# A state-space mixer on one core: the work between two sequences spread over sixteen states, and the router's statistics taken in the mixer's last sequence

## The chip, the core and the metric

The kernel runs on one core of a Trainium2 chip. Five engines work side by side, each through its own queue of instructions in order: PE (TensorE, matrix products into PSUM), DVE (VectorE), ACT (ScalarE), POOL (GpSimd) and SP (SyncE, which here only issues DMAs). The metric is the device time of one execution in microseconds.

## The reference

Eight sequences of 512 tokens, 256 wide, go through four layers; each layer is an attention-like mixer and a feed-forward part, and each part is `x = x + layernorm(part(layernorm(x)))`. The change touches the mixer of the last layer (called L3_attn), and the first step of the part after it (L3_ffn, a mixture of eight experts). The mixer, with DI = 512 channels and 16 states:

```python
xr = x @ W_in.T
xc, res = (xr[..., :DI], xr[..., DI:])
u = silu(conv1d(xc, W_conv, taps=4, causal) + b_conv)        # per channel
x_dbl = u @ W_xproj.T                                        # -> dt (16), B (16), C (16)
delta = softplus(dt @ W_dt.T + b_dt)
A = -exp(A_log)                                              # 512 x 16
dA = exp(delta * A);  dBu = delta * B * u                    # per channel and state
h_t = dA_t * h_{t-1} + dBu_t                                 # scan over the 512 tokens
y = sum over states of h * C,  + u * D
return (y * silu(res)) @ W_out.T
```

The router of L3_ffn then works on `layernorm(x)`: `softmax(xf @ w_router)`, the best two of eight experts for each token.

## The kernel before, in words

A framework orders the instructions. The program is traced in Python, and when it ends, a scheduler plays it against a model of the chip and lays down one fixed queue for each engine. An instruction that stands earlier in the Python code goes first when two are ready at the same modelled moment; one that stands much later may be pulled far forward when its engine is idle in the model. On the chip nothing is reordered: an instruction at the head of a queue waits, and everything behind it on that engine waits too. `tc.keep_in_program_order(ins)` pins an instruction behind the one traced before it on its engine, and `tc.issue_after(ins)` pins a block's instructions behind `ins`. Tiles come from pools: a tile of a tag with `bufs` buffers can be written only when the tile that used the buffer `bufs` allocations ago is no longer read.

`l3_attn` (from line 1506) goes through 8 sequences (`b`) times 16 states (`n`) in one loop. For each state:

- `inputs(b, n)` (L1603) is called two states ahead. It loads C over a DMA, and makes dB = du * B for all four channel blocks. For even n, PE spreads B over the partitions into PSUM (tile `pb`, L1610) and DVE multiplies (L1613); for odd n, B comes over a DMA and POOL multiplies (L1618).
- Four times, ACT computes dA (L1664) into one of two PSUM buffers and DVE scans (L1667) into `h`; six `h` tiles of two blocks each exist, so three states.
- POOL multiplies the two `h` tiles by C (L1670).
- PE adds the products of the state before onto four PSUM accumulators (`summed`, L1638).

All other matrix results go through the two PSUM buffers of the pool `pmm`: `pb`, the input projections `pi` (L1546), the convolution `pc` (L1560), `px` (L1570), `pd` (L1583), the transposes `pxT` (L146) and the output projection `py` (L185).

What stands between two sequences (the boundary) is traced in state n = 0 of the new one. `gate` (L1628, DVE) multiplies the four accumulators with silu(res), in the tile `sr`. `out` (L1622) calls `project_out`, whose two PSUM tiles `py` are read first by `bn_stats` (DVE), and then, after the statistics, by the four normalizing activations `yn` (L172, ACT); POOL adds the result to X (L174). Then four projections give the new `sr`, copied to SBUF by ACT (L1682), and Silu is applied (L1683). The Silu needs another table in ACT than Exp and Ln do, so a table load comes before it and `log_exp_tables` (L124) puts the first table back.

`front(b + 1)` (L1551) is a generator that is advanced once a state, from n = 0: norm and transposes, four convolutions with one yield each, the Silu of u with its two table loads (L1565), `px`, four pieces of delta (`pd`, five ACT and three DVE instructions each, L1583 to L1596), and last du = delta * u, as one POOL instruction (L1599). The tile `yn` and the normalized tile `xn` (L160) share one buffer (tag `xn`).

In `l3_ffn`, `route(b)` begins with `K.norm(b)`, whose `stats` (L99) are four `bn_stats`, four `bn_aggr` and, outside the mixer, an inverse square root of thirteen small DVE instructions (L118, L90 to L96). In the mixer (`log_exp` set) Ln and Exp on ACT and three small DVE instructions (L111 to L115) do the same.

Of the kernel before, what the change touches and what calls it, by code (L numbers as in the profile page):

```python
# [9 lines left out]
F32 = mybir.dt.float32  # L10
# [3 lines left out]
AF = mybir.ActivationFunctionType  # L14
# [5 lines left out]
P = 128  # L20
# [25 lines left out]
class Kern:  # L46


    def __init__(self, ctx, tc, i):
        self.ctx, self.tc, self.nc, self.i = ctx, tc, tc.nc, i  # L50
        nc = self.nc
        self.const = ctx.enter_context(tc.tile_pool(name="const", bufs=1))
        self.xpool = ctx.enter_context(tc.tile_pool(name="xres", bufs=1))
        self.wpool = ctx.enter_context(tc.tile_pool(name="wts", bufs=1))
        self.small = ctx.enter_context(tc.tile_pool(name="small", bufs=3))
        self.dram = ctx.enter_context(tc.tile_pool(name="dram", bufs=1, space=DRAM))
        self.C = self.const.tile([P, 384], F32, name="C")
        nc.sync.dma_start(out=self.C, in_=i["consts"][:, 0:384])
        self.ident = self.C[:, C_ID:C_ID + 128]
        self.caus = self.C[:, C_CAUS:C_CAUS + 128]  # L60
        self.up = self.C[:, C_UP:C_UP + 128]
        self.ones = self.const.tile([1, 128], F32, name="ones")
        nc.vector.memset(self.ones, 1.0)
        self.XA = self.xpool.tile([P, NB, NT, D], F32, name="X")
        self.X = [self.XA[:, b] for b in range(NB)]
        self.W = {}

        self.log_exp = False
        self.eps = self.const.tile([P, 1], F32, name="eps")
        nc.vector.memset(self.eps, LN_EPS)  # L70
# [54 lines left out]

    def norm(self, b, pool):

        nc = self.nc
        x = self.X[b]
        mv, r = self.stats([x[:, n, :] for n in range(NT)], "ln")  # L130
        xn = pool.tile([P, NT, D], F32, tag="xn", name=f"xn{b}")
# [31 lines left out]

    def add_norm(self, b, ys, pool, tag="yn"):

# [3 lines left out]
        nc.vector.scalar_tensor_tensor(nb, mv[:, :, 0], -1.0, r, ALU.mult, ALU.mult)  # L169
        t = pool.tile([P, NT, D], F32, tag=tag, name=f"yn{b}")  # L170
        for n in range(NT):
            nc.scalar.activation(  # L172
                t[:, n, :], ys[n], AF.Identity, bias=nb[:, n:n + 1], scale=r[:, n:n + 1])
        nc.gpsimd.tensor_tensor(self.X[b], self.X[b], t, ALU.add)  # L174

    def project_out(self, b, chunks, psum, ptag, pool, tag="yn"):

        nc = self.nc
        ys = []
        for half in range(2):  # L180
            ps = psum.tile([P, 2, D], F32, tag=ptag, name=f"py{b}_{half}")
            for j in range(2):
# [5 lines left out]
                ys.append(ps[:, j, :])  # L188
        self.add_norm(b, ys, pool, tag)

# [1315 lines left out]
def l3_attn(K):  # L1506

    nc, tc = K.nc, K.tc  # L1510
    w = K.W["l3_attn"]
# [4 lines left out]
    with ExitStack() as es:  # L1516
# [33 lines left out]

        def front(b, res):  # L1551
            xT = K.norm_T(
# [3 lines left out]
            for c in range(4):  # L1556
# [7 lines left out]
                yield  # L1564
            nc.scalar.activation(flat(u), flat(u), AF.Silu)  # L1565
            K.log_exp_tables()
            yield
            px = pmm.tile([48, L], F32, tag="mm", name=f"px{b}")
# [10 lines left out]

            dl = s2.tile([P, 4, L], F32, tag="dl", name=f"dl{b}")  # L1580
            for c in range(4):
                ps = pmm.tile([P, L], F32, tag="mm", name=f"pd{b}_{c}")
# [13 lines left out]
                nc.vector.tensor_tensor(dl[:, c, :], ps, dl[:, c, :], ALU.add)  # L1596
                yield
            du = s2.tile([P, 4, L], F32, tag="du", name=f"du{b}")
            nc.gpsimd.tensor_tensor(flat(du), flat(dl), flat(u), ALU.mult)  # L1599
            res.update(xT=xT, u=u, dl=dl, du=du, xd=xd,  # L1600
# [21 lines left out]
        def out(b, yT):  # L1622
            K.project_out(
                b, [(yT[:, c, :], W[:, c, M_OUT:M_OUT + D]) for c in range(4)], pmm, "mm", s1, tag="xn")

# [5 lines left out]
        def summed(state):  # L1631
# [4 lines left out]
            for j, h in enumerate(hs):  # L1636
                for c in range(2):
                    nc.tensor.matmul(  # L1638
                        py[2 * j + c], lhsT=K.ident, rhs=h[:, c, :], start=False,
                        stop=(n == NS - 1))  # L1640

# [5 lines left out]
        py = sr = last = None  # L1649
        nxt = iter(())  # L1650
        for k, (b, n) in enumerate(order):
            if n == 0:
                nxt = front(b + 1, res[b + 1]) if b + 1 < NB else iter(())
                dl, u = res[b]["dl"], res[b]["u"]
# [17 lines left out]
            if n == 0:  # L1672
                yT = gate(b - 1, py, sr) if b else None
                py = [pY.tile([P, L], F32, tag=f"y{c}", name=f"y{b}_{c}") for c in range(4)]
                for c in range(4):
                    nc.tensor.matmul(
                        py[c], lhsT=dg[:, c, 4, :], rhs=u[:, c, :], start=True, stop=False)
                if b:
                    out(b - 1, yT)
                sr = s1.tile([P, 4, L], F32, tag="sr", name=f"sr{b}")  # L1680
                for c in range(4):
                    nc.scalar.copy(sr[:, c, :], project_in(b, 4 + c, res[b]["xT"]))  # L1682
                nc.scalar.activation(flat(sr), flat(sr), AF.Silu)  # L1683
                K.log_exp_tables()
            last = (py, hs, n)
            next(nxt, None)
        summed(last)
        out(NB - 1, gate(NB - 1, py, sr))
        K.log_exp = False

def l3_ffn(K):
# [18 lines left out]
    with ExitStack() as es:  # L1712
# [60 lines left out]
        def route(b, sb):  # L1773

            xn = K.norm(b, sb)
            nc.sync.dma_start(
# [342 lines left out]
```

## Time and profile before

| what | value |
|---|---|
| runs shown | 5260.04, 5270.05 and 5273.43 us, median 5270.05 |
| profiled execution, its own time | 5271.25 us |
| its span in the profile | 5269.5 us |
| mean granted TensorE clock | 0.926 |
| busy over the span | PE 84%, DVE 57%, ACT 36%, POOL 35% |
| the mixer's first du and its last addition to X (POOL) | start 3503.6 us and 4627.0 us |

Times in the profile are microseconds from the start of the span. A line of a timeline gives the start, the duration, the engine, the line of the kernel, the operation, the tile written and those read, how many such instructions were merged, and in brackets how long the engine had been idle before it and whose end released it. The shares of busy time are averages over stages with different limits, so the mixer is read by itself below, one sequence at a time.

### The profile page before, as it was taken

The page shows a single profiled execution, that of the slowest core. Times are in us where ns is not written, and L with a number is a line of the kernel's source. Part 1 is how long each engine was busy: PE and PEld are TensorE (multiplying, and loading weights), DVE is VectorE, ACT ScalarE, POOL GpSimd, SP SyncE. Part 2 cuts the span into 40 slices and gives each one's busy share as a digit, 9 for nine tenths or more (in the row PEclk, how much of TensorE's full clock was granted, in tenths as well). Part 3 has the DMA queues.
Part 4 walks back from the last instruction along what each step waited for, and adds up shares of the span by engine and source line. Part 5 has one row for each costly group of instructions (what it writes and reads, how often), then busy time and mean ns, then how long its engine had stood idle before and what let it go on. Part 6 is the DMA issues. An engine that isn't in the chain of part 4 may idle for free.

```text
span 5269.5 us, 56453 instructions
## 1 busy us (share of the span) xinstructions
PE 4444.4 (84%) x18804; PEld 2705.9 (51%) x18804; DVE 3024.7 (57%) x8229; ACT 1886.4 (36%) x3769; POOL 1866.9 (35%) x1201
## 2 busy tenths in 40 slices
PE   8755789999983996888888889978888888899998
PEld 3334675565652994444444445533333333368885
DVE  7999646476686114454554544347777777761114
ACT  5401324443441332333333332345555555421112
POOL 0001213443442443111111110037888778903331
PEclk9777889999996997999999999989999999899999
DMA  4297411000001992000000000011111111126763
GB/s 115 78 215 161 132 49 42 5 9 5 5 17 48 251 251 59 4 5 5 5 5 4 1 1 20 1 31 45 49 46 46 43 44 46 42 86 197 233 215 102
DMA packets 401527, 357.88 MB, mean 68 GB/s; under 512 B 209394, under 2 KB 334020, under 8 KB 400676
## 3 DMA queue, kind: packets, MB, share of 16 engines
q1 hardware_dynamic: 373236, 305.83, 21.0%
q0 software_dynamic: 16320, 31.65, 2.2%
q10 hardware_dynamic: 11680, 16.80, 1.0%
q8 instruction: 149, 2.44, 0.2%
q14 instruction: 142, 1.16, 0.1%
HBM read 287.87 MB, written 66.09 MB: 67 GB/s over the span
## 4 chain that ended last, share of the span: by engine, by line
PE 38%; DVE 16%; ACT 5%; POOL 4%; issue 4%; DMA 1%; POOLq 0%; DVEq 0%; ACTq 0%; SPq 0%
DVE h L1667 7%; PE gb L1746 4%; PE T L1402 4%; PE h L1234 3%; PE S L1379 3%; PE y L1638 3%; PE g L1495 3%; PE yb L1760 2%; DVE junk L1384 2%; DVE dB L1613 2%; PE py L185 2%; PE pc L1560 2%; PE y L1245 2%; PE o L1411 2%; ACT PT L1405 1%
## 5 line engine op out<-in xcount | busy, mean ns | idle before, releaser
L1670 POOL TENSOR_TENSOR h<-h,C 128x1024 f32<-128x1024 f32 x256 | 596.0, 2358 | 177.6 <-DVE h L1667 140.5
L1638 PE MATMUL y<-h,C 128*128 128x512 f32 x1024 | 533.4, 661 | 106.7 <-POOL h L1670 106.7
L1667 DVE TENSOR_TENSOR_SCAN h<-dA,dB 128x512 f32<-128x512 f32 x512 | 588.9, 1202 | 28.4 <-ACT dA L1664 11.7
L1664 ACT ACTIVATE dA<-dl,A 128x512 f32<-128x512 f32 x512 | 352.5, 691 | 411.1 <-DVE h L1667 395.3
L1638 PEld LDWEIGHTS y<-h,C 128*128 128x128 f32 x1024 | 202.8, 209 | 413.9 <-issue 226.6
L929 POOL TENSOR_SCALAR p<-p,rs 128x128 f32<-128x128 f32 (+3 forms) x256 | 276.3, 1089 | 386.9 <-DVE rs L928 227.2
L1379 PE MATMUL S<-KT,qz 128*128 128x512 f32 (+3 forms) x1024 | 348.9, 477 | 41.7 <-ACT qz L1367 21.3
L174 POOL TENSOR_TENSOR X<-X,yn 128x1024 f32<-128x1024 f32 x64 | 151.2, 2363 | 654.8 <-ACT yn L172 593.7
L1405 ACT ACTIVATE PT<-T 128x256 f32<-128x256 f32 (+3 forms) x512 | 211.8, 437 | 387.4 <-PE T L1402 379.7
L1402 PE MATMUL T<-qz,KT 128*128 128x512 f32 (+3 forms) x1024 | 313.9, 450 | 2.9 <-DVE mx L1384 0.3
L1407 POOL TENSOR_SCALAR_AFFINE_SELECT PT<-PT 128x512 f32<-128x512 f32 x128 | 81.6, 637 | 634.0 <-ACT PT L1405 630.5
L1379 PEld LDWEIGHTS S<-KT,qz 128*128 128x128 f32 x1024 | 183.5, 197 | 209.8 <-DVE mx L1384 57.8
L1618 POOL TENSOR_TENSOR dB<-du,B 128x2048 f32<-128x2048 f32 x64 | 289.8, 4529 | 0.1
L1384 DVE CUSTOM_DVE_ANT_0 junk<-S,mask 128x256 f32<-128x256 f32 (+3 forms) x512 | 250.2, 489 | 60.8 <-PE S L1379 15.3
L1746 PE MATMUL gb<-xbT,w_b 128*128 128x256 f32 (+1 forms) x1472 | 255.3, 332 | 1.0 <-ACT ts L1950 0.6
L1613 DVE TENSOR_TENSOR dB<-du,pb 128x2048 f32<-128x2048 f32 x64 | 145.4, 2273 | 170.4 <-PE pb L1610 120.7
L1746 PEld LDWEIGHTS gb<-xbT,w_b 128*128 128x128 f32 x1472 | 230.2, 191 | 23.1 <-ACT ts L1950 0.8
L1402 PEld LDWEIGHTS T<-qz,KT 128*128 128x128 f32 x1024 | 170.7, 192 | 133.9 <-issue 85.6
L1752 DVE TENSOR_TENSOR hTb<-sb,gb 128x512 f32<-128x512 f32 x71 | 48.8, 688 | 325.4 <-PE gb L1746 325.4
L927 ACT ACTIVATE p<-p,nm 128x128 f32<-128x128 f32 (+3 forms) x256 | 143.8, 563 | 196.8 <-DVE nm L923 191.9
L1239 ACT ACTIVATE hT<-h,w_l_ffn 128x128 f32<-128x128 f32 x384 | 109.8, 368 | 220.6 <-PE h L1234 220.6
L1234 PE MATMUL h<-xgT,w 128*128 128x128 f32 x1536 | 185.3, 279 | 0.0
(503 smaller groups left out, 9045.0 us busy)
## 6 DMA issues: line engine op xcount, KB each, us to landing
w_b<-l3f_w SPq DMA_DIRECT2D x138, 512.0 KB
w<-l1f_w SPq DMA_DIRECT2D x48, 1024.0 KB
C<-xdd SPq DMA_DIRECT2D x128, 256.0 KB
B<-xdd SPq DMA_DIRECT2D x64, 256.0 KB
w<-l1f_w SPq DMA_DIRECT2D x48, 256.0 KB
toep<-l0fd SPq DMA_DIRECT2D x32, 320.0 KB
X<-x SPq DMA_DIRECT2D x16, 512.0 KB
toep<-l0fd SPq DMA_DIRECT2D x32, 256.0 KB
```

Source lines behind the costliest of these rows:

```text
L929: nc.gpsimd.tensor_scalar(p[:, 0:n], p[:, 0:n], rs, None, ALU.mult)
L1234: nc.tensor.matmul(ph[:, j, :], lhsT=w1[:, s, c, m * P:(m + 1) * P], rhs=xgT[:, c, :], start=(c == 0), stop=(c == 1))
L1379: nc.tensor.matmul(ps[:, 0:n], lhsT=QZ[:, j, qt * P:n], rhs=KT[:, g, 0:n], start=True, stop=True)
L1384: nc.vector.tensor_tensor_reduce(out=junk[:, 0:n], in0=tiles[j][:, 0:n], in1=mask[:, L - n:L], scale=1.0, scalar=-3.0e38, op0=ALU.add, op1 ...
L1402: nc.tensor.matmul(ps[:, 0:n], lhsT=KT[:, g, kt * P:(kt + 1) * P], rhs=QZ[:, j, kt * P:L], start=True, stop=True)
L1405: nc.scalar.activation(PT[:, j, :], ps[:, 0:n], AF.Exp)
L1618: nc.gpsimd.tensor_tensor(dB, du, B[:, None, :].to_broadcast([P, 4, L]), ALU.mult)
L1638: nc.tensor.matmul(py[2 * j + c], lhsT=K.ident, rhs=h[:, c, :], start=False, stop=(n == NS - 1))
L1664: nc.scalar.activation(dA, dl[:, c, :], AF.Exp, scale=A[:, c, n:n + 1])
L1667: nc.vector.tensor_tensor_scan(hs[-1][:, c % 2, :], dA, dB[:, c, :], 0.0, ALU.mult, ALU.add)
L1670: nc.gpsimd.tensor_tensor(h, h, C[:, None, :].to_broadcast([P, 2, L]), ALU.mult)
L1746: nc.tensor.matmul(ps[:, q, :], lhsT=ww[:, k, (c + q) * P:(c + q + 1) * P], rhs=xT[:, k, :], start=(k == 0), stop=(k == 1))
```

## The change

Six things are done, all in `l3_attn` but for the last.

1. The boundary's work becomes a generator, `among`, advanced once a state from n = 1 on: `out` in state 1, two of the four projections for `sr` in state 2 and two in state 3, then the pieces of `front(b + 1)` from state 4 on. `gate` and the first products onto the accumulators stay in state 0.
2. The Silu of `sr` stands directly before the Silu of u in `front`, with one return to the first table behind both. The yield behind them is gone.
3. Delta comes in two pieces to a state rather than one.
4. du is four POOL instructions of 128x512, each directly behind its piece of delta, rather than one of 128x2048.
5. The output projection's two PSUM tiles are copied to SBUF by ACT, and the normalizing activations read the copy.
6. In the last sequence, where there is no next `front`, the norm statistics that the router needs for sequences 0 to 6 are computed one to a state from state 5 on, each group behind a `memset` (the fence) that is pinned in program order, and kept in tiles of their own. `route` uses them.

```diff
+    def fence(self):
+        t = self.small.tile([P, 1], F32, tag="fence", name="fence")
+        return self.tc.keep_in_program_order(self.nc.vector.memset(t, 0.0)).ins
...
-        mv, r = self.stats([x[:, n, :] for n in range(NT)], "ln")
+        mv, r = known or self.stats([x[:, n, :] for n in range(NT)], "ln")
...
         t = pool.tile([P, NT, D], F32, tag=tag, name=f"yn{b}")
+        for n, ps in enumerate(halves):
+            nc.scalar.copy(t[:, 2 * n:2 * n + 2, :], ps)
+        if halves:
+            ys = [t[:, n, :] for n in range(NT)]
...
-            nc.scalar.activation(flat(u), flat(u), AF.Silu)
+            for t in (sr, u):
+                if t is not None:
+                    nc.scalar.activation(flat(t), flat(t), AF.Silu)
             K.log_exp_tables()
-            yield
...
-                yield
-            du = s2.tile([P, 4, L], F32, tag="du", name=f"du{b}")
-            nc.gpsimd.tensor_tensor(flat(du), flat(dl), flat(u), ALU.mult)
+                nc.gpsimd.tensor_tensor(du[:, c, :], dl[:, c, :], u[:, c, :], ALU.mult)
+                if c % 2:
+                    yield
...
+        def among(b, yT, sr):
+            if b:
+                out(b - 1, yT)
+            yield
+            sr.append(s1.tile([P, 4, L], F32, tag="sr", name=f"sr{b}"))
+            for c in range(4):
+                nc.scalar.copy(sr[0][:, c, :], project_in(b, 4 + c, res[b]["xT"]))
+                if c % 2:
+                    yield
+            if b + 1 < NB:
+                yield from front(b + 1, res[b + 1], sr[0])
+            else:
+                nc.scalar.activation(flat(sr[0]), flat(sr[0]), AF.Silu)
+                K.log_exp_tables()
+                for d in range(NB - 1):
+                    yield
+                    mv = K.const.tile([P, NT, 2], F32, name=f"fmv{d}")
+                    r = K.const.tile([P, NT], F32, name=f"fr{d}")
+                    K.known.append((mv, r))
+                    with tc.issue_after(K.fence()):
+                        m, t = K.stats([K.X[d][:, n, :] for n in range(NT)], "ln")
+                        nc.vector.tensor_copy(mv, m)
+                        nc.vector.tensor_copy(r, t)
...
-                if b:
-                    out(b - 1, yT)
-                sr = s1.tile([P, 4, L], F32, tag="sr", name=f"sr{b}")
-                for c in range(4):
-                    nc.scalar.copy(sr[:, c, :], project_in(b, 4 + c, res[b]["xT"]))
-                nc.scalar.activation(flat(sr), flat(sr), AF.Silu)
-                K.log_exp_tables()
+                sr = []
+                nxt = among(b, yT, sr)
+            else:
+                next(nxt, None)
             last = (py, hs, n)
-            next(nxt, None)
```

More of the change, by code (lines that the diff above doesn't have):

```diff
@@ L68, in __init__ @@
         self.log_exp = False
+        self.known = []
         self.eps = self.const.tile([P, 1], F32, name="eps")
@@ L124, in log_exp_tables, with norm @@
             self.nc.scalar.preload_act_table_set("natural_log_exp_and_others"))
[L126 removed]
+    def fence(self):
+        t = self.small.tile([P, 1], F32, tag="fence", name="fence")
+        return self.tc.keep_in_program_order(self.nc.vector.memset(t, 0.0)).ins
+    def norm(self, b, pool, known=None):
         nc = self.nc
         x = self.X[b]
[L130 removed]
+        mv, r = known or self.stats([x[:, n, :] for n in range(NT)], "ln")
         xn = pool.tile([P, NT, D], F32, tag="xn", name=f"xn{b}")
@@ L162, in norm_act, with add_norm @@
         return xn
-    def add_norm(self, b, ys, pool, tag="yn"):
+    def add_norm(self, b, ys, pool, tag="yn", halves=()):
         nc = self.nc
@@ L174, in add_norm, with project_out @@
         nc.gpsimd.tensor_tensor(self.X[b], self.X[b], t, ALU.add)
-    def project_out(self, b, chunks, psum, ptag, pool, tag="yn"):
+    def project_out(self, b, chunks, psum, ptag, pool, tag="yn", leave=False):
         nc = self.nc
-        ys = []
+        ys, halves = [], []
         for half in range(2):
@@ L188, in project_out @@
                 ys.append(ps[:, j, :])
-        self.add_norm(b, ys, pool, tag)
+            halves.append(ps)
+        self.add_norm(b, ys, pool, tag, halves if leave else ())
 def load_l0_attn(K):
@@ L1549, in project_in, with front @@
             return ps
-        def front(b, res):
+        def front(b, res, sr=None):
             xT = K.norm_T(
@@ L1580, in front @@
             dl = s2.tile([P, 4, L], F32, tag="dl", name=f"dl{b}")
+            du = s2.tile([P, 4, L], F32, tag="du", name=f"du{b}")
             for c in range(4):
@@ L1623, in out @@
             K.project_out(
-                b, [(yT[:, c, :], W[:, c, M_OUT:M_OUT + D]) for c in range(4)], pmm, "mm", s1, tag="xn")
+                b, [(yT[:, c, :], W[:, c, M_OUT:M_OUT + D]) for c in range(4)], pmm, "mm", s1, tag="xn",
+                leave=True)
         def gate(b, py, sr):
@@ L1649, in l3_attn @@
         py = sr = last = None
-        nxt = iter(())
         for k, (b, n) in enumerate(order):
             if n == 0:
-                nxt = front(b + 1, res[b + 1]) if b + 1 < NB else iter(())
                 dl, u = res[b]["dl"], res[b]["u"]
@@ L1672, in l3_attn @@
             if n == 0:
-                yT = gate(b - 1, py, sr) if b else None
+                yT = gate(b - 1, py, sr[0]) if b else None
                 py = [pY.tile([P, L], F32, tag=f"y{c}", name=f"y{b}_{c}") for c in range(4)]
@@ L1677, in l3_attn @@
                         py[c], lhsT=dg[:, c, 4, :], rhs=u[:, c, :], start=True, stop=False)
-                if b:
-                    out(b - 1, yT)
-                sr = s1.tile([P, 4, L], F32, tag="sr", name=f"sr{b}")
-                for c in range(4):
-                    nc.scalar.copy(sr[:, c, :], project_in(b, 4 + c, res[b]["xT"]))
-                nc.scalar.activation(flat(sr), flat(sr), AF.Silu)
-                K.log_exp_tables()
+                sr = []
+                nxt = among(b, yT, sr)
+            else:
+                next(nxt, None)
             last = (py, hs, n)
-            next(nxt, None)
         summed(last)
-        out(NB - 1, gate(NB - 1, py, sr))
+        out(NB - 1, gate(NB - 1, py, sr[0]))
         K.log_exp = False
@@ L1773, in route @@
         def route(b, sb):
-            xn = K.norm(b, sb)
+            xn = K.norm(b, sb, K.known[b] if b < len(K.known) else None)
             nc.sync.dma_start(
```

## The prediction, on record before the result

> **What bounds the kernel now.** I read the page first; then, for the mixer (3503 to 4627 us), the busy time of each engine from one addition to X (POOL, L174) to the next; then POOL's timeline for its idle time; then DVE's, ACT's and PE's where POOL stands idle. One sequence takes 143.2 us, six times alike:
>
> ```profile
> 3807.07:3950.27 143.20, 124.33 (x276) 50.63 (x274) 107.71 (x114) 75.93 (x115) 116.81 (x44) 0.92 0.17 45
> 3950.27:4093.43 143.16, 122.82 (x274) 50.03 (x272) 107.60 (x114) 75.94 (x115) 116.78 (x43) 0.93 0.15 45
> ```
>
> The columns are the stretch, its length, then busy us (and count) of PE, PE's weight loads, DVE, ACT and POOL, and the granted clock. No engine is full; PE (123) and POOL (117) are nearest. POOL's 116.8 is 32 products with C, 8 of dB, one du and one addition to X. Where nothing disturbs it, in the last sequence, it is the bound: busy 73.80 of the 73.80 us from 4539.6 to 4613.4, two states every 13.7 us. So I ask where POOL's other 26.4 us of a sequence go:
>
> ```profile
> 3945.62 4.65 POOL L1670 TENSOR_TENSOR h<-h,C 128x1024 f32<-128x1024 f32 x2 [2.78 <-DVE onb L169]
> ...
> 3975.19 9.28 POOL L1670 TENSOR_TENSOR h<-h,C 128x1024 f32<-128x1024 f32 x4 [18.14 <-DVE h L1667]
> ```
>
> 18.14 us are one hole at each boundary (18.14 to 18.22 in all six), 2.78 a second, and 5.5 lie in pieces of 1 to 1.5. DVE's timeline shows what the scans of the hole waited for:
>
> ```profile
> 3940.83 2.03 DVE L113 SCALAR_TENSOR_TENSOR onh<-onmv,ony 128x4 f32<-128x4 f32 x1 [0.60 <-ACT ony L112]
> ...
> 3952.60 1.41 DVE L105 BATCH_NORM_STATS2 lnst<-X 128x6 f32<-128x256 f32 x4 [4.91 <-POOL X L174]
> 3955.67 1.39 DVE L115 SCALAR_TENSOR_TENSOR lnw<-lnh,lny 128x4 f32<-128x4 f32 x1 [1.67 <-ACT xn L160]
> ...
> 3970.30 2.29 DVE L1613 TENSOR_TENSOR dB<-du,pb 128x2048 f32<-128x2048 f32 x1 [12.01 <-PE pb L1610]
> ```
>
> dB of state 4 stands 12.01 us for `pb`, one matrix product whose inputs are long there. It is late because `pmm` has two buffers and everything of the boundary was traced ahead of it: two `py`, four `pi`, two `pxT`, a `pi`, a `pc`. The `py` are held until `yn` has read them (3946.05 to 3947.96), and `xn` waits for the addition to X, which reads the buffer it shares with `yn`. The bn_stats in the list are the router's, for the X just finished, pulled forward out of L3_ffn.
>
> **Part 1 and 5, the order and the copy.** After the change only `py` stands before `pb` of state 4; two `pi` come behind it, then two more in state 3, `pb` of state 6, `pxT`. The `py` are free once the bn_stats (until 3940.01 in this row) and two copies of 0.59 us (128x512 from PSUM, L1682) are done, 7 us sooner than 3947.10, when the first `pi` started. Then `pb` needs no yn, no xn, no transpose. I take the whole hole as gone: -18.1 us in six sequences. ACT pays 1.2 us for the copies and has 67 us idle in the row: nothing, and 1.2 a sequence should that cover fail. The copies wait for PE at the head of ACT's queue with the dA behind them; the same queue waits 3.8 us for `pc` today (L1563) and POOL loses 1.5 there, so I count that among the 5.5 us that stay. The 2.78 stays too: it comes from L113. Bounds for the hole: nothing, if another wait fills it (rivals), and 26.4 if all idle time goes.
>
> **What must then carry the work.** PE was not idle in the hole: busy 17.45 us of the 17.70 from 3957.5 to 3975.2, at clock 1.00. That work moves and stays. Its room is where PE waits for POOL at the end of a sequence:
>
> ```profile
> 4010.00:4030.00 20.00, 18.20 (x39) 6.79 (x40) 19.83 (x20) 14.46 (x25) 18.89 (x8) 1.00 0.20 61
> 4030.00:4050.00 20.00, 14.44 (x27) 4.91 (x26) 13.89 (x14) 8.77 (x14) 18.53 (x6) 0.85 0.16 47
> 4050.00:4070.00 20.00, 14.35 (x20) 5.01 (x20) 18.05 (x15) 7.52 (x11) 18.63 (x9) 0.67 0.17 51
> ```
>
> There the clock falls to 0.67 and eight products take 6.7 us instead of 3.70. The row's 128 products of L1638 are 67.3 us busy; at 3.70 for eight they would be 59.2, so PE's own need is 122.8 - 8.1 = 114.7 us, just under POOL's.
>
> **Part 4, du in four.** POOL's 128x1024 takes 2.36 us and 128x2048 4.50, so 128x512 is some 1.28 and four are 5.1: +0.6 a sequence. In the first front nothing hides du (DVE waits 4.78 us for it at 3508.14); there only the last piece counts: 4.50 - 1.28 = -3.2 us, once.
>
> **Part 2 and 3, Silu and delta.** A Silu costs ACT 1.28 (load) + 1.91 + 1.28 (load). Joined with the other it saves one pair of loads, 2.6 us of ACT in a row with 67 idle, but blocks dA 6.4 us in one piece rather than 4.5 twice. Nothing pins `sr`'s Silu, which is ready in state 4, so the scheduler may well put it early by itself; then all loads stay. Either way between -1 and +2 a row; I take 0. Delta's four pieces need the same 8.1 us of DVE; in two states DVE then needs 2 x 4.5 for scans, 2.2 for dB and 8.1 = 19.3 against POOL's 13.7. POOL can eat its lead of a state; I leave that within the 5.5. `front` takes one DMA along, xd to memory on SP's queue (issued at 4009.25), from state 6 to 9. C loads that wait up to 22.4 us for POOL stand before it there; the next sequence reads it from state 14, five states or 34 us on: nothing, and the excess over 34 if SP lags more.
>
> The Trainium skill (ScalarE: Activation LUTs, What ACT_TABLE_LOAD costs) adds a drain of about 1.38 us to each load; in this trace Silu follows the load after 0.01 us and the return load follows the Silu at once, so no drain shows, and seven joined pairs would be worth 18 us of ACT by the rows, 37 by the page, none of it on the path.
>
> **Part 6, the router's statistics.** In the mixer they leave six boundaries (1.4 us of bn_stats each, behind a wait in the hole, counted with it) and enter the last sequence, seven groups in states 5 to 11. A group is 1.4 + 0.4 (bn_stats, bn_aggr) + three instructions of 0.16, two copies of about 0.1 and a memset: 2.5 us of DVE, 17.5 in all. L113 shows what may come on top: seven times out of seven it took 1.93 to 2.22 us rather than 0.16, ending as POOL's running instruction ended (3942.86 against 3942.84). One such wait a group: 7 x (2.5 + 2.0) = 31.5 us. Against it, DVE's slack over three and a half pairs of states, 3.5 x (13.7 - 11.2) = 8.8, and one state of lead, 5.6. So the last sequence grows by 17, and loses the 4.98 of its own boundary: **+12**. Bounds: -5 with no wait at all; with all five small instructions waiting for a whole 2.36 us product, 7 x (2.5 + 11.8) - 14 - 5 = +81. I stay near the L113 row, since a POOL that runs dry blocks nobody.
>
> By the Trainium skill (SBUF, two separate sides), DVE with two SBUF inputs or in its two-port mode and POOL exclude each other for a whole instruction. L113 agrees. Read strictly it speaks against this part: each of the five could wait, which is the +81 above.
>
> In L3_ffn DVE is relieved of some 11 us between 4616 and 4676, but PE is busy 57.36 of the 63.00 us from 4613.4 to 4676.4 and full behind it. What can be gained is PE's wait of 4.56 us before the first `pxT`, for a `yn` that holds PSUM: **-4** (0 to -5.6).
>
> **Sum**, against the profiled execution's own 5271.25 (1.2 above the median of the runs shown, so the median would be as much lower): 6 x (-18.1 + 0.6) = -105; first front -3; last sequence +12; router -4; total -100, **5171 us**. A sequence would take 125.7 us.
>
> **Rivals.**
>
> *PE becomes the bound* (0.17). The boundary and `front` are 46 us of PE (pi 14.8, pc 14.7, px 3.6, pd 4.5, pxT 1.2, py 7.2), now in states 1 to 11, whose own products and `pb` need 11 x 4.3 = 47.5: 93.5 us where POOL needs 75.4. Six `h` tiles let POOL run two states, 13.7 us, ahead. Then five states remain, of which POOL has done two: 20.5 + du 5.1 + X 2.3, plus PE's last state 4 and the gate's 3: 128.4 a sequence, -14.8 x 6 = -89; with the other terms **5187**.
>
> *All idle time closes* (0.13): only the 2.8 stays, 120.2 a sequence, -138, and the statistics cost nothing: -5 -3 -4, **5121**.
>
> *The gain is mostly eaten* (0.08): delta's burst and the ACT block cost POOL 8 us a row, the last sequence +30: -57 + 23 = **5237**.
>
> *The change doesn't do what it says* (0.06): the scheduler pulls the pieces back to where they were as soon as an engine is idle in its model, and `pb` queues as before: -3 +12 -4, **5276**.
>
> *Slower: du comes late* (0.16). Today dB of the next sequence's state 0 already waits:
>
> ```profile
> 4045.76 4.49 POOL L1599 TENSOR_TENSOR du<-dl,u 128x2048 f32<-128x2048 f32 x1
> ...
> 4050.29 2.29 DVE L1613 TENSOR_TENSOR dB<-du,pb 128x2048 f32<-128x2048 f32 x1 [6.40 <-POOL du L1599]
> ```
>
> That wait costs POOL 1.37. `front` now starts at state 4 rather than 0, up to 21 us later, and wins back two states, 14. A `pd` holds its buffer from 4007.8 to 4019.5, so four in two buffers take 23.4 us, from state 10 to past 13. DVE's queue holds dB, and the scans of states 14 and 15 behind it, and POOL those of the products. Beyond some 5 us each further us costs one a sequence; beyond 23 us of lateness the 17.5 is gone. At 30 us late: 6 x 7.5 + 5 = **5321**.
>
> **Numbers.** Forecast 0.40. Faster by over 0.3% (16 us, about what a measurement of this kernel can tell): 0.40 + 0.17 + 0.13 + 0.08 = 0.78; within 0.06; slower 0.16. The range goes from just under the best case to the eaten gain, 5115 to 5245; outside are the last two rivals, 0.22.
>
> **What would show it.** Right: POOL's idle time of 18 us before L1670 is gone in all six sequences; dB waits for `pb` under 3 us at state 4; 125 us from X to X; clock at a sequence's end above 0.8. PE bound: PE over 95% busy in a sequence, POOL waiting for L1638. Late du: an idle time on DVE before L1613 by du, over 10 us. Statistics: L113 to L115 of 2 us in the last sequence, which takes over 95 us from its X to the last product with C. Wrong would be my figure if POOL's hole only moves.

## The result and the profile after

The changed kernel takes 5299.29 us (median of 7 runs) where the kernel before takes 5265.07 (7 runs beside it): 1.0056 times as long, with a 95% interval of 1.0038 to 1.0074. It is slower by 0.56%. The forecast was 5171 with a range of 5115 to 5245; sign and range were wrong. The profiled execution took 5296.40 us, its span is 5294.7 (before: 5271.25 and 5269.5), so the two traces differ by 25.2.

Executions of programs that are alike up to the mixer differ by up to 22 us where it begins, and the addition to X moved by a state. So I count from the first product with C of one sequence to the first of the next (POOL's 32 products with C a sequence, read off its timeline):

| stretch, us | before | after | difference | forecast |
|---|---|---|---|---|
| start to the first product with C | 3515.0 | 3511.1 | -3.9 | -3 |
| first sequence | 123.1 | 127.6 | +4.5 | not thought of |
| six sequences between, together | 859.9 | 853.0 | -6.9 | -105 |
| last sequence, to its last product | 115.4 | 139.9 | +24.5 | +12 |
| from there to the end | 656.1 | 663.1 | +7.0 | -4 |

The two large misses are the six sequences, which won 7 us and not 105, and the last one. That the first row comes so near to its forecast is in part luck: the mixer's first `dg` instruction (the weights of the convolution) starts at 3437.7 us before and at 3434.8 after, so 2.9 of the 3.9 us lie ahead of the mixer.

Here are the busy times of two sequences of the kernel after, from one addition to X (now L185) to the next; columns as in the prediction (length, then busy us and count of PE, PE's weight loads, DVE, ACT and POOL, then the clock):

```profile
3672.84:3814.06 141.22, 122.36 (x272) 50.03 (x272) 108.28 (x102) 77.00 (x118) 117.52 (x46) 0.93 0.16 45
3956.50:4099.35 142.85, 122.93 (x272) 50.36 (x272) 107.85 (x102) 77.08 (x118) 117.58 (x47) 0.93 0.15 45
```

PE and POOL do the same work at the same clock, and stand idle nearly as long as before (20 and 25 us of a sequence, where it was 20 and 26). What POOL waited for in one such sequence, first in the trace of before, then after (us in total, times, longest):

```profile
POOL h L1670 <- DVE h L1667: 22.5, 4, 18.1
POOL h L1670 <- DVE onb L169: 2.8, 1, 2.8
```

```profile
POOL h L1709 <- DVE h L1706: 21.5, 10, 3.9
POOL h L1709 <- DVE onb L176: 1.3, 1, 1.3
```

The 18.1 is gone in all six sequences, as foreseen. The total is not: 22.5 us in four waits became 21.5 in ten. They lie behind one another in the middle of the sequence. POOL's timeline of the kernel after, where the last column is the idle time before the row and what ended it:

```profile
3987.51 4.65 POOL L1709 TENSOR_TENSOR h<-h,C 128x1024 f32<-128x1024 f32 x2 [1.67 <-DVE h L1706]
3995.83 4.65 POOL L1709 TENSOR_TENSOR h<-h,C 128x1024 f32<-128x1024 f32 x2 [3.67 <-DVE h L1706]
4000.44 4.51 POOL L1633 TENSOR_TENSOR dB<-du,B 128x2048 f32<-128x2048 f32 x1
4008.87 6.97 POOL L1709 TENSOR_TENSOR h<-h,C 128x1024 f32<-128x1024 f32 x3 [3.92 <-DVE h L1706]
...
4027.39 2.36 POOL L1709 TENSOR_TENSOR h<-h,C 128x1024 f32<-128x1024 f32 x1 [3.58 <-DVE h L1706]
```

DVE's timeline shows what the scans (L1706) waited for in the same stretch:

```profile
3982.52 2.29 DVE L1628 TENSOR_TENSOR dB<-du,pb 128x2048 f32<-128x2048 f32 x1 [3.86 <-PE pb L1625]
...
3993.26 4.57 DVE L1706 TENSOR_TENSOR_SCAN h<-dA,dB 128x512 f32<-128x512 f32 x4 [3.76 <-PE y L1654]
4003.92 2.29 DVE L1628 TENSOR_TENSOR dB<-du,pb 128x2048 f32<-128x2048 f32 x1 [6.08 <-PE pb L1625]
...
4022.43 2.29 DVE L1628 TENSOR_TENSOR dB<-du,pb 128x2048 f32<-128x2048 f32 x1 [5.61 <-PE pb L1625]
```

Each is a wait for PE: for `pb`, or for the y sums that free an h buffer. And PE is full there, at full clock, while behind it, at the sequence's end, it is as idle and cold as before:

```profile
3970.00:4030.00 60.00, 57.62 (x134) 22.83 (x133) 37.40 (x31) 32.05 (x48) 44.61 (x17) 1.00 0.16 45
```

```profile
4050.00:4070.00 20.00, 12.74 (x18) 4.82 (x19) 17.08 (x16) 6.92 (x10) 17.00 (x7) 0.70 0.13 39
```

In those 60 us POOL works 44.6 and loses 15.4. The hole was cut into pieces and set down further along.

Of the other rows shown of before: the first 128x4 instruction behind Exp, which had taken 2.03, does not wait, but two behind it do, 4.6 us together. This is DVE's timeline of the kernel after at the boundary:

```profile
3946.01 0.14 DVE L114 SCALAR_TENSOR_TENSOR onh<-onmv,ony 128x4 f32<-128x4 f32 x1
...
3947.20 3.38 DVE L115 SCALAR_TENSOR_TENSOR onh<-onh,ony 128x4 f32<-128x4 f32 x1
...
3951.64 1.24 DVE L116 SCALAR_TENSOR_TENSOR onw<-onh,ony 128x4 f32<-128x4 f32 x1
```

And dB, which had waited 6.40 us for du, now waits 0.2 (DVE's waits in the same sequence):

```profile
DVE dB L1628 <- PE pb L1625: 16.8, 5, 6.1
...
DVE dB L1628 <- POOL du L1612: 0.2, 1, 0.2
```

### The profile page after: what moved, and what is told of

Same layout as the page of the kernel before. It is cut to its first block, busy times and chain, and to the rows that moved or that the text cites. A ratio compares the mean times of both kernels' runs of the same rounds, so it can differ in the third digit from the quotient of the medians.

```text
span 5294.7 us, 56486 instructions
## 1 busy us (share of the span) xinstructions
PE 4453.8 (84%) x18804; PEld 2710.1 (51%) x18804; DVE 3063.0 (58%) x8180; ACT 1898.0 (36%) x3799; POOL 1871.5 (35%) x1225
## 4 chain that ended last, share of the span: by engine, by line
PE 37%; DVE 15%; ACT 6%; issue 5%; POOL 4%; DMA 1%; POOLq 0%; DVEq 0%; SPq 0%; ACTq 0%
DVE h L1706 6%; PE gb L1781 4%; PE T L1414 4%; PE h L1246 3%; PE S L1391 3%; PE g L1507 3%; PE y L1654 3%; PE yb L1795 2%; DVE junk L1396 2%; DVE dB L1628 2%; PE py L196 2%; PE pc L1573 2%; PE y L1257 2%; PE o L1423 1%; ACT PT L1417 1%
## 5 line engine op out<-in xcount | busy, mean ns | idle before, releaser
L1706 DVE TENSOR_TENSOR_SCAN h<-dA,dB 128x512 f32<-128x512 f32 x512 | 591.4, 1204 | 84.5 <-PE y L1654 35.5
L1654 PE MATMUL y<-h,C 128*128 128x512 f32 x1024 | 545.2, 671 | 89.9 <-POOL h L1709 89.6
L185 POOL TENSOR_TENSOR X<-X,yn 128x1024 f32<-128x1024 f32 x64 | 151.2, 2362 | 652.9 <-ACT yn L183 591.9
```

What stands on the lines that cost most here:

```text
L1654: nc.tensor.matmul(py[2 * j + c], lhsT=K.ident, rhs=h[:, c, :], start=False, stop=(n == NS - 1))
L1706: nc.vector.tensor_tensor_scan(hs[-1][:, c % 2, :], dA, dB[:, c, :], 0.0, ALU.mult, ALU.add)
```

## The experiments

Three theories stood after the traces. **P**: PE sets the pace of the states that hold a piece of `front`, so the hole was PE's work and could only move. **Q**: waits of the queues in order, and of DVE for POOL's running instructions, set it, with PE having room. **S/W**: the statistics made the last sequence long, by their waits for POOL rather than by their work. All ratios are to the kernel before, run beside each kernel; "first", "six" (the mean of the six middle sequences) and "last" are read from the profiled execution. That execution is not always a typical one: it lies 17 us above its kernel's median in e1, 14 in e2 and 12 in e3, and 10 under it in e12, 17 in e13 and 18 in e10. The kernel before had medians from 5265.07 to 5277.69 beside the others, so kernels that did not run side by side (e1 to e4; e5, e6, e8 and e9; e10 to e13; e14 to e16; e17 and e18 did) are compared by their ratios.

| kernel | median us | ratio, 95% interval | first | six | last |
|---|---|---|---|---|---|
| before | 5265.07 | 1 | 123.1 | 143.3 | 115.4 |
| after | 5299.29 | 1.0056 (1.0038-1.0074) | 127.6 | 142.2 | 139.9 |
| e1 no statistics | 5286.31 | 1.0030 (1.0019-1.0042) | 127.7 | 147.1 | 111.5 |
| e2 statistics only | 5304.57 | 1.0055 (1.0042-1.0067) | 123.6 | 144.1 | 144.1 |
| e3 more PE early | 5333.55 | 1.0109 (1.0093-1.0125) | 134.1 | 153.7 | 111.0 |
| e4 more PE late | 5302.56 | 1.0048 (1.0031-1.0065) | 127.6 | 147.4 | 112.9 |
| e5 bare statistics | 5263.18 | 0.9985 (0.9975-0.9994) | 128.2 | 142.5 | 115.2 |
| e6 gate late | 5252.59 | 0.9965 (0.9952-0.9979) | 120.8 | 141.9 | 117.3 |
| e9 gate late, front in state 4 | 5248.95 | 0.9958 (0.9945-0.9971) | 127.6 | 139.8 | 115.9 |
| e8 no refining | 5253.75 | 0.9970 (0.9959-0.9981) | 127.6 | 141.3 | 107.9 |
| e10 gate late, xn apart | 5240.60 | 0.9935 (0.9922-0.9948) | 120.8 | 137.5 | 115.9 |
| e12 xn apart only | 5268.96 | 0.9984 (0.9975-0.9993) | 135.9 | 140.0 | 116.1 |
| e11 one tap | 5170.13 | 0.9791 (0.9779-0.9804) | 118.7 | 130.4 | 116.3 |
| e13 no copy | 5271.86 | 0.9995 (0.9983-1.0008) | 127.7 | 142.4 | 114.7 |
| e16 before, one tap | 5232.43 | 0.9919 (0.9903-0.9934) | 118.5 | 138.8 | 116.3 |
| e14 front spread | 5223.66 | 0.9911 (0.9898-0.9925) | 125.8 | 133.2 | 117.6 |
| e15 spread, no refining | 5208.72 | 0.9889 (0.9874-0.9904) | 125.7 | 133.0 | 110.6 |
| e17 spread evenly | 5181.90 | 0.9829 (0.9816-0.9843) | 118.7 | 129.7 | 114.3 |
| e18 evenly, no refining | 5141.18 | 0.9758 (0.9738-0.9778) | 118.7 | 123.2 | 114.0 |

### The statistics: e1, e2, e5

e1 takes part 6 out of the changed kernel.

```diff
-                for d in range(NB - 1):
-                    yield
-                    ...
-                        nc.vector.tensor_copy(r, t)
```

> The changed kernel without its part 6 (the router computes its own statistics, as before). Counted from the first product with C of one sequence to that of the next, the last sequence grew from 115.4 to 139.9 us, and the stretch from the last product to the end from 656.1 to 663.1. Theory S, the statistics are the loss: the last sequence goes back to 116 to 121 us and the end to 656 to 659, so 5268 to 5275 us in all, level with the kernel before. Rival, the last sequence is long because the boundary's pieces now lie in it: it stays above 130, and the time above 5288.

The last sequence fell to 111.5, as theory S said, but the time only by 0.26% (the difference of the ratios), not to the level of the kernel before. The surprise is the six sequences: 147.1, five longer than with part 6. (That is the profiled execution, 17 us above the median; by the ratios some 16 of the 29 us that the last sequence and the end gave back were lost elsewhere, 2.6 a sequence.) DVE's timeline of e1, just behind the addition to X, shows why; these are 128x4 instructions of the router's statistics, pulled to the boundary as in the kernel before:

```profile
3688.70 2.24 DVE L119 TENSOR_SCALAR lnv<-lnmv 128x4 f32<-128x4 f32 x1
3690.97 4.44 DVE L91 TENSOR_SCALAR lny<-lnv 128x4 int32<-128x4 int32 x1
3695.33 0.16 DVE L93 TENSOR_SCALAR lnh<-lnv 128x4 f32<-128x4 f32 x1
```

0.16 is such an instruction's own time; 2.24 and 4.44 hold waits for what POOL was running: the first ends at 3690.94, POOL's product with C at 3690.92, the second at 3695.41, POOL's dB at 3695.39. In the kernel before the same instructions lay inside POOL's 18 us hole and cost nothing. Over the six sequences of e1, the small instructions that took over 0.3 us add up to 13.0, 13.4, 13.4, 14.1, 5.2 and 4.7 us; the sequences take 148.2, 147.5, 148.2, 153.8, 142.8 and 141.8. So part 6 did earn something in the new order: it was cheap before only because the hole was there.

e2 gives the kernel before part 6 alone, in the same states:

```diff
+        def late():
+
+            for _ in range(4):
+                yield
...
-                nxt = front(b + 1, res[b + 1]) if b + 1 < NB else iter(())
+                nxt = front(b + 1, res[b + 1]) if b + 1 < NB else late()
```

> The kernel before with part 6 alone: statistics of the seven finished X in states 5 to 11 of the last sequence. Theory S, they cost by themselves what the last sequence and the end gained, 24.5 + 7: 5285 to 5297 us. Rival, they cost only where the boundary's pieces crowd the same states: within 8 us of the kernel before.

The last sequence takes 144.1 rather than 115.4, and the whole 0.55% more: by themselves the statistics cost what the changed kernel lost. Its six sequences do not shorten; in the kernel before the hole hid them there.

e5 keeps bn_stats and bn_aggr in those states and does the rest once, after the last product:

```diff
+                        for n in range(NT):
+                            nc.vector.bn_stats(st[:, n, :], K.X[d][:, n, :])
+                        for n in range(NT):
+                            nc.vector.bn_aggr(mvs[:, d, n, :], st[:, n, :])
...
+            nc.scalar.activation(y, var, AF.Ln, bias=K.eps)
...
+        K.known = [(mvs[:, d], r[:, d]) for d in range(NB - 1)]
```

> The changed kernel, with only bn_stats and bn_aggr of the seven finished X in states 5 to 11 of the last sequence (bn_aggr straight into a tile that stays); Ln, Exp, the refining and the factors come once for all seven, behind the last product with C. Without statistics the last sequence takes 111.5 us, with them 139.9. Theory W, the small instructions with two SBUF operands and the copies wait for POOL and make the 28: the last sequence takes 112 to 119, the six before it stay at 142, and the time falls 20 to 28 under the changed kernel, level with the kernel before or up to 8 above. Rival, it is the statistics' work and fences, whatever their form: 130 or more, less than 10 gained.

Theory W held: the last sequence takes 115.2, 24.7 less than after, and the time is 0.15% under the kernel before, by the ratios some 37 us under the changed kernel where 20 to 28 were expected. DVE's timeline of the kernel after shows what went: one group's small instructions, between scans of 1.21.

```profile
4569.54 4.36 DVE L114 SCALAR_TENSOR_TENSOR lnh<-lnmv,lny 128x4 f32<-128x4 f32 x1
4573.83 0.16 DVE L1681 COPY fmv<-lnmv 128x8 f32<-128x8 f32 x1
...
4575.03 0.13 DVE L115 SCALAR_TENSOR_TENSOR lnh<-lnh,lny 128x4 f32<-128x4 f32 x1
...
4576.22 1.48 DVE L116 SCALAR_TENSOR_TENSOR lnw<-lnh,lny 128x4 f32<-128x4 f32 x1
...
4578.75 0.14 DVE L1682 COPY fr<-lnw 128x4 f32<-128x4 f32 x1
```

Of 35 such instructions in the seven groups 11 took 0.4 us or more, 25.7 us together; the longest, 3.5 to 4.6, end with one of POOL's dB (4.5). POOL then stands dry until DVE is free again:

```profile
4585.36 2.34 POOL L1709 TENSOR_TENSOR h<-h,C 128x1024 f32<-128x1024 f32 x1 [3.99 <-DVE lnw L116]
```

The other 24 met a POOL that stood idle or had just ended. bn_stats (0.42) and bn_aggr never waited, in e5 or after. From here on e5 is the base.

### Does PE set the pace? e3, e4, e11, e16

e3 and e4 add products with zero weights to e1, early or, with `(12, 14)`, late:

```diff
+            if n in (5, 7):
+                for c in range(4):
+                    nc.tensor.matmul(py[c], lhsT=zero, rhs=win[:, 0, 0:L], start=False, stop=False)
```

> The changed kernel without part 6, and in states 5 and 7 of each sequence four more products of 128x512 into the y sums, with weights of zero, so that the sums stay what they are: 3.7 us of PE each by the y sums' row at clock 1.00, 7.4 us a sequence. Theory P, TensorE sets the pace of states 1 to 11 and the hole only moved: each of eight sequences grows by 6 to 7.4 us, 48 to 59 over the kernel without statistics. Rival Q, those states are paced by waits for evictions and for DVE's shared port, with PE having room between: under 15.

> The same extra products, but in states 12 and 14, where PE waits for POOL at a low clock. Theory P: this work finds room there, -10 to +10 against the kernel without statistics (below it if the busier PE is granted a higher clock). Rival Q: the same, so this one serves as the other half of the pair: early minus late is 40 to 60 by P, within 15 by Q.

Early, the 7.4 us of PE lengthened the sequences by 6.6 (first: 6.4), 47 us between the medians. Late, they lengthened them by 0.3; the medians differ by 16 and the ratios by 0.18% (9 us), most of which the sequences do not show. Early minus late is 31 us between the medians, neither the 40 to 60 of P nor the 15 of Q; by the sequences of the two traces it is 6.3 in each of the six, as P says. In the last sequence, which has no `front`, the early ones cost nothing either (111.0 against 111.5). Of the places tried, PE paces those with `front`, and no other.

e11 takes 11 us of `front`'s products out of e5:

```diff
-                for s in range(4):
-                    nc.tensor.matmul(
-                        pc, lhsT=dg[:, c, s, :], rhs=xc[:, 3 - s:3 - s + L],
-                        start=(s == 0), stop=(s == 3))
+                nc.tensor.matmul(pc, lhsT=dg[:, c, 0, :], rhs=xc[:, 3:3 + L], start=True, stop=True)
```

> As the kernel with bare statistics, but the convolution of front leaves out three of its four taps (12 products a sequence, 11.0 us of PE by the row of pc). Theory P for states 4 to 10: this work lies where PE paces, so each sequence that has a front behind it falls by 8 to 11 us, 55 to 75 in all. Rival Q: the waits between pi, xc, pc and u stay, and under 20 is gained.

The six fell by 12.1 each and the first by 9.5, 82.1 us together, a little more than the products' own 77; the time fell by 1.9%, the difference of the ratios, some 100 us where 55 to 75 were expected. Q is out for these states.

> The kernel before, with three of the four taps of front's convolution left out (12 products a sequence, 11.0 us of PE). Theory P, the hole of 18 us was PE working off the boundary and front at full clock: the hole shrinks by 2 to 8 us (of the taps, those that lie in it) and a sequence falls by 8 to 12, as it did in the changed kernel with bare statistics (12). Rival, the hole was the order of a queue whose buffers were held: it stays at 16 to 18, and a sequence falls by less than 5.

The same edit in the kernel before. POOL's hole, in e16's timeline:

```profile
3953.63 6.97 POOL L1667 TENSOR_TENSOR h<-h,C 128x1024 f32<-128x1024 f32 x3 [15.57 <-DVE h L1664]
```

It shrank by 2.6: one `pc` of the four lay in it, whose three missing products are 2.76 us. So the hole consisted of PE's work, as P says. But a sequence fell only by 4.5, not by P's 8 to 12; that half went as the rival said (under 5). The other nine products, 8.3 us, brought some 2: outside the hole they lay where PE had room. In the changed order, by e11, all twelve lie where it has none.

### Moving PE's work: e6, e9, e10, e12, e13

In e6 the projections of sr go behind `front`:

```diff
+            if b + 1 < NB:
+                yield from front(b + 1, res[b + 1])
             sr.append(s1.tile([P, 4, L], F32, tag="sr", name=f"sr{b}"))
             for c in range(4):
                 nc.scalar.copy(sr[0][:, c, :], project_in(b, 4 + c, res[b]["xT"]))
...
-                yield from front(b + 1, res[b + 1], sr[0])
```

> As the kernel with bare statistics, but the four projections of sr come behind the next sequence's front (states 10 and 11 in place of 2 and 3, their Silu alone in state 12, xT in two buffers, lg in one). Eight products of 0.92 us leave the crowded states for those where PE waits for POOL. Theory P, TensorE sets the pace of the crowded states: each sequence but the last falls by 5.5 to 7.4 us, 38 to 52 under the kernel with bare statistics. Rival Q, waits set it: within 12 of it.

In e9 two more `yield`s stand ahead of `yield from front`.

> As the kernel with the gate late, but front starts in state 4 again, two states empty before it. Theory P: the same products in fewer states with room, so between the two others, 10 to 40 under the kernel with bare statistics, and du later by up to 14 us. Rival Q: within 12 of the kernel with bare statistics.

Against e5 the medians fell by 10.6 us in e6, which is Q's figure (within 12) and not P's 38 to 52, and by 14.2 in e9, inside P's 10 to 40 but not between e5 and e6, as P had it. The first sequence fell by 7.4 in e6, just the eight products, but the six by 0.6 only, and by 2.7 in e9. What PE waits for in one sequence of e6:

```profile
PE pxT L152 <- ACT xn L166: 8.2, 1, 8.2
PE y L1654 <- POOL h L1709: 7.0, 3, 3.7
```

In the like sequence of e5, PE waits 8.0 us for sr's copies there and not for `xn`. So the time that PE gained in states 2 and 3 went into waiting for `xn`, which waits for the addition to X (they share a buffer), which waits for yn, the output's statistics and their waits for POOL. In e9 this wait is 13.0. The first sequence has no such boundary ahead of it. So P alone was not enough: a sequence is a chain that must end, then `front` at PE's pace, then POOL's rest. This is theory C. e10 breaks the chain in e6 by putting `xn` into sr's buffer; e12 gives it a buffer in e5 (`tag="xq"`, and `s1` in place of `s2` for `e` and `lg`). The cut shows one argument of a longer call, as e10 has it:

```diff
-xn=K.norm_act(b, s1)
+xn=K.norm_act(b, s1, s1.tile([P, 4, L], F32, tag="sr", name=f"xq{b}")[:, :, 0:D])
```

> As the kernel with the gate late, and xn of the next sequence lies in the buffer of sr, which is free then, in place of the one that it shares with yn; so it waits no longer for the addition to X. In the kernels with the gate late PE waits 8.2 and 13.0 us in a sequence for xn, at the head of the crowded stretch. Theory C, this chain (statistics of the output, yn, addition to X, xn, transposes) sets when front may start, and a sequence is chain, then front at PE's pace, then POOL's rest: the sequences fall by 6 to 12 us, 35 to 75 in all, to 5180 to 5215. Rival, PE's idle time only shows up at another wait, as it has done so far: within 12 us of the kernel with the gate late.

> As the kernel with bare statistics, with a buffer of its own for xn and the gate's projections left in states 2 and 3 (the room comes from one buffer each for e and lg). Theory C: the projections fill the wait for xn here, so little is won, 0 to 4 us a sequence, 0 to 28 in all, and only both together give the whole. Rival, xn's wait alone is the loss: as much as both together.

e10: the six fall by 4.4 each, less than the 6 to 12, and that in an execution 18 us under the median; the time falls by 0.30% by the ratios, some 16 us where 35 to 75 were expected, little more than the rival's 12. e12: nothing (0.9984 against 0.9985), although three of its six sequences are 3 to 5 us shorter; its first is 8 us longer. The direction is that of theory C, the size is half or less.

e13 undoes part 5 in e5:

```diff
-                leave=True)
+                leave=False)
```

> As the kernel with bare statistics, without part 5: yn is read from PSUM as before, so the two buffers stay held until the statistics of the output, with their waits for POOL, are done. If the copies are worth what the prediction took (7 us earlier for what stands behind): 4 to 7 us a sequence slower, 25 to 45 in all. Rival, what stands behind would wait for xn anyway: within 10.

0.10% slower than e5, with overlapping intervals; the six are level (142.4 and 142.5). In the order of e5 the copies are worth nothing that can be measured, as the rival said.

### Spreading it: e14, e17, and the refining: e8, e15, e18

e14 is e10 with the same work: `front` starts one state earlier and its four pieces take eight states. e17 also starts it in state 0, gives delta four states as the kernel before does, and puts one projection of sr behind each piece of delta. Of the cut, the first `yield` is in both, the rest in e17 alone.

```diff
                 nc.scalar.copy(xc[:, 3:], project_in(b, c, xT))
+                yield
                 pc = pmm.tile([P, L], F32, tag="mm", name=f"pc{b}_{c}")
...
-                if c % 2:
-                    yield
+                if side:
+                    side(c)
+                yield
```

> As the kernel with xn apart, but front starts in state 1, right behind the output's projection, and its four pieces pi and pc lie in states of their own, eight states instead of four. No work is taken out. Theory crowding, PE paces the states that hold a whole piece (4.3 of its own and 5.5 us of the piece against POOL's 6.85): with 4.3 and 1.8 to 3.7 a state PE and POOL are level, and a sequence takes 126 to 132 us rather than 137.5, 40 to 75 less in all. Rival, PE's total and its cold clock behind a full POOL set the sequence: within 15 of the kernel with xn apart.

> As the kernel with the front spread, with every piece one state earlier (the first in state 0), delta in four states, and one projection of sr behind each of its pieces in place of two in each of two states after it. Theory crowding: the waits of 3 to 5 us in states 11 to 15 shrink, and a sequence takes 126 to 130 us rather than 133.2, 20 to 45 less in all. Rival, PE's total and its cold clock are the limit now: within 12.

e14 brought 133.2, a little above the 126 to 132. Its time fell by 0.24% against e10, some 13 us, where 40 to 75 were expected; that is inside the rival's 15. What POOL still waits for lies at the sequence's end, in state 14 and before the first product of the next sequence, as its timeline of e14 shows:

```profile
4022.84 2.35 POOL L1710 TENSOR_TENSOR h<-h,C 128x1024 f32<-128x1024 f32 x1 [3.36 <-PE y L1656]
...
4042.08 2.35 POOL L1710 TENSOR_TENSOR h<-h,C 128x1024 f32<-128x1024 f32 x1 [5.34 <-PE y L1656]
```

There delta and sr's projections stand close together. PE is not full there (busy 14.1 of the 20 us from 4008.9), so this is not PE's crowd alone: POOL also waits 3.1 us for a piece of delta.

e17 brought 129.7 in every one of the six (126 to 130 were expected), 0.82% under e14 and 1.7% under the kernel before. It computes all that the kernel before computes. PE's busy time is nearly that of the kernel after (121.2 against 122.6 us a sequence); only its place is another.

e8, e15 and e18 take the refining (the three small DVE instructions behind Ln and Exp) out of e5, e14 and e17:

```diff
-            nc.scalar.activation(y, y, AF.Exp, scale=-0.5)
-            nc.vector.scalar_tensor_tensor(t, var, LN_EPS, y, ALU.add, ALU.mult)
-            nc.vector.scalar_tensor_tensor(t, t, -0.5, y, ALU.mult, ALU.mult)
-            nc.vector.scalar_tensor_tensor(r, t, 1.5, y, ALU.add, ALU.mult)
+            nc.scalar.activation(r, y, AF.Exp, scale=-0.5)
```

> As the kernel with bare statistics, but the mixer's norms take Exp(-Ln/2) itself as factor: the three refining steps, which wait up to 4.8 us each for POOL at every boundary, are left out there. Theory P, PE paces the crowded states, and what DVE waits is caught up: within 2 us a sequence, -14 to +5 in all. Rival Q, these waits are what took the hole's place: 4 to 6 us a sequence, 28 to 42 less than with bare statistics.

> As the kernel with the front spread, but the mixer's norms take Exp(-Ln/2) itself as factor, without the three refining steps. If the boundary's waits for POOL are what is left: 3 to 6 us a sequence, 20 to 40 in all under the spread one. Rival, they are caught up: within 12 of it, as 9 were gained from the kernel with bare statistics, of which 7 lay in the last sequence.

> As the kernel spread evenly, but the mixer's norms take Exp(-Ln/2) itself as factor, without the three refining steps. Without the crowd the boundary's waits for POOL should count as in the last sequence, where leaving them out won 7: 2 to 7 us a sequence, 15 to 45 in all. Rival, they stay hidden: within 12 of the kernel spread evenly, and these lie in the last sequence.

Under PE's crowd the refining's waits are worth little: 1.2 us a sequence in e8 (within the 2 of P) and 0.2 in e15 (under the 3 to 6 looked for), and 7 in the last sequence, where there is no crowd. In e17 there is little of it left, and without refining a sequence falls by 6.5 to 123.2, inside the 2 to 7 expected, 2.4% under the kernel before. (The last sequence of e18 gains 0.3 only; why is open.) One sequence each of e17 and e18:

```profile
3885.60:4015.30 129.70, 121.24 (x272) 50.62 (x272) 105.78 (x103) 76.55 (x118) 117.50 (x45) 0.93 0.17 50
```

```profile
3879.40:4002.60 123.20, 114.97 (x272) 48.63 (x272) 103.46 (x99) 76.45 (x119) 117.36 (x45) 0.99 0.18 52
```

The same 272 products are 6.3 us shorter, at a clock of 0.99 rather than 0.93. The small instructions of e17's boundary took only 2.8 us where they waited (0.49 and 2.31). The trace shows how more can come of it: ACT's `yn` waits 2.93 us for the second of them, a copy of `xT` stands behind `yn`, and PE waits 2.63 us for that copy, until 3910.93. From 3910 to 3920 the clock is 0.54 and 0.50 (two stretches of 5 us); in e18 PE waits 0.75 at this place and the clock stays at 1.00. That the rest of the 6.5 comes from the clock fits these rows, but no run sets the clock by itself; it is argued, not shown.

## Why the prediction was wrong, step by step

- **"I take the whole hole as gone: -18.1 us in six sequences."** As a line of the profile it is gone, as time it is not: 22.5 us of waits for scans became 21.5. The row that told it was in the prediction: PE was busy 17.45 of the hole's 17.70 us at full clock. This hole, in which PE was full, was PE's work (e16).
- **"Its room is where PE waits for POOL at the end of a sequence."** This step failed. The room is there, but the work did not go there. e3 and e4 measure it: 7.4 us of PE cost 6.6 early and 0.3 late. A state with a whole piece of `front` needs 4.3 + 5.5 = 9.8 us of PE against POOL's 6.85, and the changed order puts four such states, px and delta behind one another.
- **PE becomes the bound** (0.17, 128.4 a sequence) was the right mechanism with a wrong sum. It let PE run through states 1 to 11 without a wait. In fact PE stood waiting at the boundary (in the sequence from 3922.4 of the kernel after 4.0 us before a `pb` and 2.8 before `pi`, both for sr's copies), then was full, then idle and cold: busy 122.6 of 142.8 us.
- **Parts 2 and 3, Silu and delta**, counted as 0: part 2 did not come about in any sequence. As the prediction had thought possible, sr's Silu ran by itself (at 3966.45 in the same sequence) and u's later (4015.74), each between two loads of 1.28 us. No run takes part 3 alone; e17, which gives delta its four states back, changes more than that.
- **Part 4, du in four**: DVE's wait in the first front fell from 4.78 to 1.37 us, 3.4 where -3.2 was said. Right, and du was never late: the rival with the right sign named the wrong mechanism.
- **Part 5, the copies**: e13 shows them to be worth nothing measurable in the order of e5, not the 7 us earlier start for which they were counted.
- **Part 6, "the last sequence grows by 17"**: by 24.5 here, 28.7 in e2. "One such wait a group", 14 us in all, was the mis-sized term: 11 waits took 25.7, four of them behind a dB of 4.5 us, not behind a product of 2.36. "A POOL that runs dry blocks nobody" missed that POOL itself is the bound there. The Trainium skill (SBUF — State Buffer, section SBUF: two separate sides) counts every DVE instruction with two SBUF inputs, or in a two-port mode, as excluded while one of POOL's that reads SBUF runs; read so, all five of a group may wait, the +81 of the prediction for the last sequence. Eleven of 35 did; the others met a POOL that the wait before had left dry (L115 at 4575.03 starts between POOL's products, which end at 4573.88 and start again at 4575.34). The measured +24.5 lies between the two estimates, +12 and +81, nearer to the prediction's.
- **Part 6 at the boundary** was "counted with it", the hole. e1 shows what it was worth once the hole had gone: five us a sequence in the profiled execution, 2.6 as reckoned from the ratios.
- **The router, -4**: the end took 663.1, but 655.5 to 662.7 in the other kernels, with and without part 6 (e2 658.5, e1 662.1). No gain is seen; how much of +7 belongs to the change stays open.
- **The first sequence**, +4.5, was not in the sum: it has no boundary ahead, so the pieces of sr and `front` only crowd there. Taking sr's projections away (e6) gave 7.4 back.
- The sign to look for was named right: "Wrong would be my figure if POOL's hole only moves."

## What to carry to other kernels

Before a hole on the bounding engine is counted as a gain, look at who is full inside it: here it was PE's work, and it went away only when it was placed where PE waits. So ask of each state what every engine needs there, not only over the whole round. Giving `xn` another buffer and spreading the same pieces over the states brought a sequence from 142.5 to 129.7 us and left no operation out; 7.8 of this came with the spreading (137.5 to 129.7). And small DVE instructions that are free beside an idle POOL can each wait for the rest of a POOL instruction once POOL is kept busy: 11 of 35 did, 2.3 us each on average.

## What the runs showed of the hardware

- A 128x4 TENSOR_SCALAR on DVE with a single tensor as input took 2.24 and 4.44 us beside a busy POOL (e1), and a 128x4 COPY up to 1.49 (after), against 0.16 beside an idle one; bn_stats (at most 0.43 a piece), bn_aggr (at most 0.19) and the fences' memset (0.06) never did so in any run. It is not only instructions with two inputs.
- The same 272 products of a sequence took PE 122.6 us at a mean granted clock of 0.93 (after), 121.2 at 0.93 (e17), 117 to 118 at 0.96 to 0.97 (e14) and 115.0 at 0.99 (e18). It is not evenness alone: e17 is laid more evenly than e14 and had the lower clock. In e17 one wait of PE of 2.63 us was followed by some 10 us at half the clock.
